# Seven block products for queries, keys and values, in a planned two-layer graph kernel

## The chip, the cores and the metric

The kernel runs on one core of a Trainium2 chip. The metric is device time in microseconds. The engines are named as in the profile: PE is TensorE (matmuls, with PEld for its weight loads), DVE is VectorE, ACT is ScalarE, POOL is GpSimd, and SP is SyncE, which here issues all DMAs.

## The reference

There are 64 graphs of 256 nodes with 256 features, all in float32, and an adjacency matrix for each. Two layers follow each other.

```
layer 0:  two graph attentions (softmax over axis 1 of masked pairwise scores, times h @ W),
          residual, layer norm, feed-forward 256 -> 1024 -> 256 with ReLU, residual, layer norm
layer 1:  q, k = x @ Wq + bq, x @ Wk + bk             (8 heads of 32)
          out = sum over r of (softmax(q k^T / sqrt(32)) * (adj == r)) @ (x @ Wv[r] + bv[r])
          x = LN(x + out @ Wo + bo);  x = LN(x + gelu(x @ W1 + b1) @ W2 + b2)
```

The adjacency holds only 0 and 1, so only two of the four value matrices matter.

## The kernel before

The graphs are taken in 32 pairs. `whole_way(pair)` is a Python generator that emits the instructions of one pair: `gat_layers` (both graph attentions), `feed_forward` stage 0, `attention`, `feed_forward` stage 2, and the store. What reaches PE is cut into steps: each `yield` names the events that the next step needs, what it must hold alone ("gat", "ff", "attention"), and how many PSUM banks and other buffers it takes. Work for the other engines is given to `put(engine, us, emit, *events, rank=..., needs=..., frees=...)`.

`run(reliefs(), ways, 3)` is a planner. It keeps a clock for each engine, costs that are written beside each piece, and lists of when buffers come free (`free`). With three pairs in flight it always emits the piece that can start first; on PE it prefers a step that has been ready for 0.5 us, oldest pair first. `keep_order` then pins each engine to the emitted order. So the order is fixed when the program is built, and each engine is an in-order queue: an instruction that waits holds up all behind it on its engine. The true waits are semaphores.

The lines that matter below, by the work they do:

- L409, L425, L438: matmuls of the graph attentions; L400 and L380 evacuate and scale on ACT.
- L589: first half of the feed-forward network. `Slabs` computes a product of 2 x 2 blocks with seven block products (the Winograd form of Strassen's scheme) in place of eight. For two slabs of 128 rows it uses three banks: `x` collects products 1, 6, 7 and 4, and is copied out by ACT (L595) after 1, 6 and 7; `w` holds product 2, `z` products 5 and 3. DVE adds at L601, and makes the sums of input blocks at L560. L576 is the activation.
- L674: second half of the feed-forward network; L451, L463 to L479: residual and layer norm, with the root on POOL (L469, L470) and the normalisation on ACT (L474).
- L499, L504, L510: the rows are turned into columns by a DVE transpose into `yb`, a store and four gathers. In the first and last pairs ("hurried") PE does it (L530, L534).
- L695: queries and keys, two matmuls of 512 columns each for two halves of the features. L687: values, in the same way for each half of a graph. L696 and L689 evacuate with the bias.
- L728: scores by head; L735 exp on ACT; L739 and L743 mask and add halves on DVE; L757 and L760 products with the values and the sums of the softmax; L769 and L770 divide; L766 adds the divisor and its reciprocal up into `reach`, a check of the range that is read at the end.
- `load(pair)` starts DMAs for xT, the adjacency and x of the next pair. The adjacency becomes bytes on ACT (L393) and gives a maximum on DVE (L396).
- `relieve`, `relieve_values` and `block_sums` prepare biases and block sums of weights once, at the start.

If the check of ranges failed, `any_inputs` would do everything anew by another way; with these inputs it doesn't run.

Of the kernel before, what the change touches and what calls it, by code (L numbers as in the profile page):

```python
# [10 lines left out]
F32 = mybir.dt.float32  # L11
# [7 lines left out]
P = 128  # L19
# [9 lines left out]
BY_BLOCKS = (0, 2)  # L29
# [4 lines left out]
def two_layers(ctx: ExitStack, tc: tile.TileContext, t: dict, out: bass.AP, flag: bass.AP):  # L34
# [37 lines left out]
    reach = const.tile([P, NPAIR, 2 * KC], F32, name="reach")  # L72
# [49 lines left out]
    small = ctx.enter_context(tc.tile_pool(name="small", bufs=4))  # L122
# [3 lines left out]
    def bank():  # L126
# [12 lines left out]
    free = {name: [0.0] * n for name, n in (("bank", 8), ("a", 2 * HQ), ("m", 2 * HQ), ("h", 2 * HQ), ("yb", 2), ("yT", 2), ("yTa", 1),  # L139
                                             ("xT", 1), ("rows", 1), ("e", 2), ("adjT", 1), ("adj", 3), ("sums", 1), ("x", 4))}  # L140
# [69 lines left out]
    def run(besides, ways, together):  # L210
# [5 lines left out]
        while True:  # L216
# [8 lines left out]
            for n, (way, events, name, banks, *more) in enumerate(going):  # L225
                if alone.get(name) in (None, way) and all(e.time is not None for e in events):
                    at = begins(max([e.time for e in events], default=0.0), "bank" if banks else None, banks)
                    for needs in more:
                        at = None if at is None else begins(at, needs)
                    if at is not None:  # L230
                        times.append((at, n))
# [8 lines left out]
            if engine == "tensor":  # L240
                sure = [n for at, n in times if at <= now - SLACK]
                g = going[min(sure, key=lambda n: (going[n][2] == "ff" or alone.get("ff") is going[n][0], n))
                          if sure else min(times)[1]]
                if g[2]:
                    alone[g[2]] = g[0]
# [32 lines left out]
    def load(pair, at=None):  # L278

        to, rows = {}, slice(2 * pair, 2 * pair + 2)  # L280

        def xT():
            to["xT"] = io.tile([P, KC, 512], F32, name="xT")
            nc.sync.dma_start(to["xT"], t["xT"][pair].rearrange("(c p) b n -> p c (b n)", p=P))

        def adjT():
            if pair == 1:
                to["adjT"] = work.tile([P, 2, 2 * D], F32, name="v", bufs=2).bitcast(I32).rearrange(
                    "p b (c n) -> p (b c) n", c=2)
            else:  # L290
                to["adjT"] = io.tile([P, 4, N], I32, name="adjT")
            nc.sync.dma_start(to["adjT"], t["adjT"][rows].rearrange("b (c p) n -> p (b c) n", p=P))

# [3 lines left out]

        if at is None:
            return to, [put("sync", 0.45, emit, rank=3, lag=2.3, kb=512, needs=emit.__name__) for emit in (xT, adjT, x)]
        for emit in (xT, adjT, x):  # L300
            takes(emit.__name__, pair == 0 or emit is x)
            emit()
        return to, [at_time(at)] * 3
# [56 lines left out]
    def gat_weights(y, at, at_home, ratio, there, to, empty, b):  # L360
# [3 lines left out]
        def weigh(j):  # L364
# [7 lines left out]
            nc.vector.scalar_tensor_tensor(e[:, j], to["adj"][:, k], empty[:, k:k + 1], e[:, j],  # L372
# [13 lines left out]
    def gat_layers(pair, to, loads):  # L386
        yield loads[:1], "gat", 2
        empty = small.tile([P, 4], F32, name="empty")
        y = work.tile([P, 4, D + 4], F32, name="xw", bufs=2)

        def small_adj():
            to["adj"] = io.tile([P, 4, N], U8, name="adj", bufs=3)
            nc.scalar.activation(to["adj"], to["adjT"], AF.Copy)  # L393

        def largest():
            nc.vector.tensor_reduce(most[:, pair], to["adjT"].bitcast(U32), axis=AX.X, op=ALU.max)  # L396
            nc.vector.tensor_scalar(empty, most[:, pair], 0.0, EVEN, ALU.is_le, ALU.mult)
# [5 lines left out]
        emptied = put("vector", 1.35, largest, put("scalar", 1.2, small_adj, loads[1], needs="adj"), rank=2, frees=["adjT"] * (pair != 1))  # L403
# [10 lines left out]
        frees_at(clock["tensor"], ["xT"] * (pair > 0))  # L414
        at_home, ratio, there = yield from addends(y, there, D + 2, 0, pair)
        e = [gat_weights(y, D + 2, at_home, ratio, [emptied, *there], to, empty, b) for b in range(2)]
# [14 lines left out]
        e = [gat_weights(z, D, at_home, ratio, there, to, empty, b) for b in range(2)]  # L431
        normal = {}
        for b in range(2):
            yield [e[b][1]], None, 1
# [54 lines left out]
    def transposed(y, ready, to, b, pair, stage):  # L489
# [6 lines left out]
        def turn():  # L496
            nonlocal blocks
            blocks = work.tile([P, 8, 2, 32], F32, name="yb", bufs=2)
# [40 lines left out]
    def feed_forward(y, normal, w, func, relieved, gb, pair, stage):  # L539

# [3 lines left out]
        half, by_blocks = NF // 2, stage in BY_BLOCKS  # L546
        sums = p2 = None
        f, evacuated = [], [[None] * NF for _ in range(2)]

        def block(c, k):  # L550
            return normal["yT"].rearrange("p b a (c k i) -> p c k (b a) i", c=KC, k=2)[:, c, k]

        def sum_of_blocks(n):
            nonlocal sums
            if n == 0:
                sums = work.tile([P, 3, N], F32, name="sums_yT")
            t1, t2, t4 = (sums[:, n].rearrange("p (a i) -> p a i", i=32) for n in range(3))
            to, of, less = ((t1, block(0, 1), block(0, 0)), (t2, block(1, 1), t1),
                            (block(0, 1), block(1, 1), block(0, 1)), (t4, block(1, 0), t2))[n]
            nc.vector.tensor_tensor(to, of, less, ALU.subtract)  # L560

        if hurried(pair, stage):
            yield from transposed_on_tensor(y, normal)
        if by_blocks:
            summed = [put("vector", 0.34, lambda: sum_of_blocks(0), normal[0], normal[1], rank=0, needs="sums")]
            for n in range(1, 4):
                summed.append(put("vector", 0.34, lambda n=n: sum_of_blocks(n), summed[-1], rank=0))

        def slabs():

            tile = work.tile([P, 2, 512], F32, name="ff", bufs=NF // 2)
            f.extend(tile[:, n] for n in range(2))
            return tile

        def activate(to, p, m, us, *events, rank=0, frees=()):
            return put("scalar", us, lambda: nc.scalar.activation(to, p, func, bias=b1[:, m:m + 1]), *events, relieved,  # L576
                       rank=rank, function=kind, frees=frees)

        class Slabs:

            def __init__(self, t):
                self.t, self.bank, self.there = t, {}, {}

            def product(self, n, to, of, rhs, first=False):

                if first:
                    self.bank[to] = bank().rearrange("p (n c) -> p n c", n=2)
                for n in range(2):
                    nc.tensor.matmul(self.bank[to][:, n], lhsT=w1[:, of, (self.t + n) * P:(self.t + n + 1) * P], rhs=rhs(),  # L589
                                     start=first and n == 0, stop=True, skip_group_check=True)  # L590
                return took(0.86)

            def evacuate(self, name, rows, at, event):
                def copy():
                    nc.scalar.activation(self.rows[rows][:, :, at], self.bank["x"], AF.Copy)  # L595
                self.there[name] = put("scalar", 0.5, copy, event, rank=-1)

            def add(self, name, rows, at, bank, *events, frees=()):
                def add():
                    to = self.rows[rows][:, :, at]  # L600
# [756 lines left out]
```

## Time and profile before

| | |
|---|---|
| median of 3 runs | 3093.85 us (3093.08 to 3093.98) |
| profiled execution | 3093.45 us, span 3091.7 us |
| granted clock of PE | 0.995 |
| DMA | 205.6 MB, mean 67 GB/s |

A row of the page's groups reads: line, engine, operation, written tile <- read tiles, shape and count, then busy time, the mean of one in ns, and the idle time just before them with what ended it. A matmul of float32 data appears as two records. "Busy" counts a moment once if any instruction of the engine runs.

### The profile page before, as it was taken

What the parts mean: (1) busy time and instruction counts of PE and PEld (TensorE: products, weight loads), DVE (VectorE), ACT (ScalarE), POOL (GpSimd) and SP (SyncE); (2) the same over time, 40 slices, a digit from 0 to 9 for tenths busy, and PEclk for the clock granted to TensorE, in tenths of its full rate; (3) what the DMA queues carried; (4) which work ended last, traced back from release to release, by engine and by line L of the source; (5) the groups of instructions that cost most, each with busy time, mean ns of one, the idle gap of its engine ahead of it and who ended that gap; (6) DMA issues with size and microseconds to landing.
All of it is one profiled execution on the core that took longest, in us unless ns stands there. A gap on an engine that the chain in (4) does not pass through costs nothing. (4 is left out here: it accounts for less than half of the span.)

```text
span 3091.7 us, 50645 instructions
## 1 busy us (share of the span) xinstructions
PE 3052.6 (99%) x18366; PEld 2309.3 (75%) x18366; DVE 2465.3 (80%) x5917; ACT 1622.4 (52%) x3452; POOL 265.9 (9%) x518
## 2 busy tenths in 40 slices
PE   7999999999999999999999999999999999999997
PEld 6777876886687778668867876786688678767856
DVE  5788888878887878888788878888887888788775
ACT  4455654653565456546545654564465456545534
POOL 0001100000010001001000100010010001000100
PEclk8999999999999999999999999999999999999999
DMA  6112311230132123113201311231132113112200
GB/s 193 38 37 65 123 35 42 90 103 29 62 101 64 35 69 117 38 39 97 95 33 58 104 61 35 76 110 44 33 102 90 35 56 110 55 40 64 69 1 15
DMA packets 210496, 205.63 MB, mean 67 GB/s; under 512 B 22208, under 2 KB 169792, under 8 KB 210240
## 3 DMA queue, kind: packets, MB, share of 16 engines
q1 hardware_dynamic: 210240, 202.32, 20.3%
q8 instruction: 148, 2.42, 0.3%
q14 instruction: 108, 0.88, 0.1%
HBM read 137.51 MB, written 64.73 MB: 65 GB/s over the span
## 5 line engine op out<-in xcount | busy, mean ns | idle before, releaser
L474 ACT ACTIVATE x<-x,less,rstd 128x256 f32<-128x256 f32 x512 | 279.1, 593 | 416.0 <-POOL less L470 414.6
L735 ACT ACTIVATE a<-ps 128x512 f32<-128x512 f32 x512 | 272.3, 603 | 395.2 <-PE ps L728 395.1
L674 PE MATMUL ps<-w_L_gnn_w_ff,ff 128*128 128x256 f32 x2048 | 462.6, 381 | 0.0
L674 PE MATMUL ps<-w_L_gnn_W,ff 128*128 128x256 f32 x2048 | 458.7, 380 | 1.7 <-ACT ff L576 1.7
L469 POOL TENSOR_TENSOR rstd<-rstd,mhalf 128x2 f32<-128x2 f32 x256 | 206.2, 806 | 2797.2 <-DVE less L466 2598.4
L674 PEld LDWEIGHTS ps<-w_L_gnn_w_ff,ff 128*128 128x128 f32 x2048 | 386.5, 190 | 70.8 <-issue 20.7
L674 PEld LDWEIGHTS ps<-w_L_gnn_W,ff 128*128 128x128 f32 x2048 | 388.2, 190 | 66.4 <-issue 12.9
L739 DVE TENSOR_TENSOR m<-a,adj 128x512 f32<-128x512 f32 x512 | 349.9, 683 | 81.8 <-ACT a L735 80.5
L595 ACT ACTIVATE ff<-ps 128x512 f32<-128x512 f32 x384 | 223.4, 590 | 220.9 <-PE ps L589 220.2
L769 DVE RECIPROCAL s<-ps 128x256 f32<-128x256 f32 x128 | 224.4, 1753 | 139.2 <-PE ps L760 139.1
L601 DVE TENSOR_TENSOR ff<-ps,ff 128x512 f32<-128x512 f32 x384 | 249.0, 681 | 26.4 <-PE ps L589 19.7
L589 PE MATMUL ps<-yT,w_L_gnn_W1p 128*128 128x256 f32 x1024 | 248.3, 386 | 4.5 <-ACT a L735 2.0
L687 PE MATMUL ps<-wv,yTa 128*128 128x512 f32 x512 | 238.7, 599 | 0.0
L589 PE MATMUL ps<-yT,w_L_gnn_w_ff1p 128*128 128x256 f32 x1024 | 238.3, 381 | 0.3 <-ACT ff L595 0.2
L451 DVE TENSOR_TENSOR x<-ps,x 128x512 f32<-128x512 f32 x256 | 174.7, 683 | 71.8 <-PE ps L674 42.6
L589 PEld LDWEIGHTS ps<-yT,w_L_gnn_W1p 128*128 128x128 f32 x1024 | 192.2, 191 | 46.1 <-ACT ff L595 5.7
L589 PEld LDWEIGHTS ps<-yT,w_L_gnn_w_ff1p 128*128 128x128 f32 x1024 | 193.3, 190 | 30.9 <-DVE x L451 3.3
L463 DVE BATCH_NORM_STATS2 st<-x 128x6 f32<-128x256 f32 x512 | 209.3, 409 | 5.5
L743 DVE TENSOR_TENSOR h<-a 128x256 f32<-128x256 f32 x512 | 213.5, 417 | 0.0
L400 ACT ACTIVATE xw<-ps 128x260 f32<-128x260 f32 (+1 forms) x256 | 96.7, 388 | 171.6 <-PE ps L425 91.4
L687 PEld LDWEIGHTS ps<-wv,yTa 128*128 128x128 f32 x512 | 94.7, 190 | 120.3 <-issue 120.1
L589 PE MATMUL ps<-sums_yT,w_L_gnn_w_ff1p 128*128 128x256 f32 x768 | 180.6, 381 | 0.4 <-DVE sums_yT L560 0.4
(118 smaller groups left out, 4743.6 us busy)
## 6 DMA issues: line engine op xcount, KB each, us to landing
home<-yb SPq DMA_DIRECT2D x182, 256.0 KB, 2.0
yT<-home SPq DMA_DIRECT2D x728, 64.0 KB, 2.0
rows<-row SPq DMA_DIRECT2D x60, 512.0 KB, 3.9
xT<-in_xT SPq DMA_DIRECT2D x32, 512.0 KB, 3.7
x<-in_x SPq DMA_DIRECT2D x32, 512.0 KB, 4.1
out<-x SPq DMA_DIRECT2D x32, 512.0 KB, 2.9
adjT<-in_adjT SPq DMA_DIRECT2D x31, 512.0 KB, 4.1
w_L_gnn_w_ff1p<-in_L_gnn_w_ff1p SPq DMA_DIRECT2D x4, 256.0 KB, 5.6
```

What stands on the lines that cost most here:

```text
L463: nc.vector.bn_stats(st[:, j, :], rows[j])
L469: nc.gpsimd.tensor_tensor(rstd, rstd, mhalf[:, :2], ALU.pow)
L474: nc.scalar.activation(rows[j], rows[j], AF.Identity, bias=less[:, j:j + 1], scale=rstd[:, j:j + 1])
L589: nc.tensor.matmul(self.bank[to][:, n], lhsT=w1[:, of, (self.t + n) * P:(self.t + n + 1) * P], rhs=rhs(), start=first and n == 0, stop=Tru ...
L595: nc.scalar.activation(self.rows[rows][:, :, at], self.bank["x"], AF.Copy)
L601: nc.vector.tensor_tensor(to, self.bank[bank], to, ALU.add)
L674: nc.tensor.matmul(p2[:, j * D:(j + 1) * D], lhsT=f[m][:, (2 * j + b) * P:(2 * j + b + 1) * P], rhs=w2[:, m, :], start=m == 0, stop=m == N ...
L687: nc.tensor.matmul(ps, lhsT=yT[:, b, c, jc * P:(jc + 1) * P], rhs=wv[:, c].rearrange("p r m -> p (r m)"), start=c == 0, stop=c == KC - 1)
L735: nc.scalar.activation(a[n][o], ps[o], AF.Exp)
L739: nc.vector.tensor_tensor(m[n][o], a[n][o], adj, ALU.mult)
L743: nc.vector.tensor_tensor(h[n][o], a[n][o][:, :N], a[n][o][:, N:], ALU.add)
L769: there = put("vector", 1.68, lambda: nc.vector.reciprocal(s, po[:, N:]), there, rank=0)
```

## The change

Queries and keys are now one 2 x 2 block product, values another, both by the seven-product scheme that the feed-forward network uses. The scheme moves into two classes: `Second` makes the sums of the input's blocks (the fourth one in place, once both readers of the block have run), `Blocks` holds the seven steps. Its fifth product goes into the bank of the second one after C11 has been read out, so two slabs need four banks and not six. Four pairs are in flight in place of three. xT and the adjacency share one input buffer, adjacency first. `yb` has one buffer in place of two, the small tiles three in place of four. The check of ranges moves from DVE to ACT, and the divisor takes the place of a tile `h`.

```diff
-    small = ctx.enter_context(tc.tile_pool(name="small", bufs=4))
+    small = ctx.enter_context(tc.tile_pool(name="small", bufs=3))
...
-    free = {name: [0.0] * n for name, n in (("bank", 8), ("a", 2 * HQ), ("m", 2 * HQ), ("h", 2 * HQ), ("yb", 2), ("yT", 2), ("yTa", 1),
-                                             ("xT", 1), ("rows", 1), ("e", 2), ("adjT", 1), ("adj", 3), ("sums", 1), ("x", 4))}
+    free = {name: [0.0] * n for name, n in (("bank", 8), ("a", 2 * HQ), ("m", 2 * HQ), ("h", 2 * HQ), ("yb", 1), ("yT", 2), ("yTa", 1),
+                                             ("input", 1), ("rows", 1), ("e", 2), ("adj", 4), ("sums_yT", 1), ("sums_yTa", 1), ("x", 4))}
...
+        def in_bytes(there):
+            return put("vector", 1.35, largest, put("scalar", 1.2, small_adj, there, needs="adj", rank=2), rank=2)
...
         if at is None:
-            return to, [put("sync", 0.45, emit, rank=3, lag=2.3, kb=512, needs=emit.__name__) for emit in (xT, adjT, x)]
+            adj = in_bytes(there(adjT, needs="input"))
+            return to, [there(xT, adj), adj, there(x, needs="x")]
...
+    class Second:
...
+        def add(self, n):
+            if n == 0:
+                self.sums = work.tile([P, 2, N], F32, name=self.name)
+            b, (t1, t2) = self.b, (self.sums[:, n].rearrange("p (a i) -> p a i", i=32) for n in range(2))
+            to, of, less = ((t1, b(0, 1), b(0, 0)), (t2, b(1, 1), t1), (b(0, 1), b(1, 1), b(0, 1)), (b(1, 0), b(1, 0), t2))[n]
+            nc.vector.tensor_tensor(to, of, less, ALU.subtract)
...
+    class Blocks:
...
+        def product(self, n, to, a, first=False):
+            if first:
+                self.bank[to] = self.bank[to] if n == 5 else bank().rearrange("p (n c) -> p n c", n=2)
+            for slab in range(2):
+                self.multiply(self.bank[to][:, slab], slab, a, self.second.of(n),
+                              start=first and slab == 0, stop=True, skip_group_check=True)
+            return took(0.86)
...
+        def p1(self):
+            yield *self.first, 1
+            self.begin()
+            self.u1 = self.copy(0, 0, self.product(1, "x", 0, True))
+        def p2(self):
+            yield [], None, 1
+            there = self.product(2, "z", 1, True)
+            self.c11 = self.add(0, 0, "z", self.u1, there)
+            self.second.read_by_second(there)
+        def p5(self):
+            yield [self.c11, self.second.there[0]], None, 0
+            self.fifth = self.product(5, "z", 2, True)
+            self.add_fifth()
+        def p6(self):
+            yield [self.u1, self.second.there[1]], None, 0
+            self.u2 = self.copy(0, 1, self.product(6, "x", 3))
+        def p7(self):
+            yield [self.u2, self.second.there[2]], None, 0
+            self.u3 = self.copy(1, 1, self.product(7, "x", 4))
+            self.add_fifth()
...
+        def p4(self):
+            yield [self.u3, self.second.there[3]], None, 0
+            self.corner(self.bank["x"], self.product(4, "x", 6))
+        def p3(self):
+            yield [self.c22], None, 0
+            self.add(0, 1, "z", self.u2, self.product(3, "z", 5), frees=["bank"])
...
-            blocks = work.tile([P, 8, 2, 32], F32, name="yb", bufs=2)
+            blocks = work.tile([P, 8, 2, 32], F32, name="yb")
...
-            for step in (a.p1, b.p1, a.p2, a.p6, b.p6, a.p5, b.p5, a.p7, b.p7, b.p2, a.p4, b.p4, a.p3, b.p3):
+        for step in (a.p1, b.p1, a.p2, a.p6, b.p2, b.p6, a.p5, a.p7, b.p7, b.p5, a.p4, b.p4, a.p3):
...
+        def multiply_qk(to, n, a, b, **flags):
+            nc.tensor.matmul(to, lhsT=wqk[:, a, n * P:(n + 1) * P], rhs=b, **flags)
+        def multiply_v(to, jc, a, b, **flags):
...
+            nc.tensor.matmul(to, lhsT=b[:, jc * P:(jc + 1) * P], rhs=wv[:, a], **flags)
...
             def check():
-                nc.vector.scalar_tensor_tensor(s, po[:, N:], 1.0, s, op0=ALU.mult, op1=ALU.add,
-                                               accum_out=reach[:, pair, n:n + 1])
+                for of, c in ((s, 0), (po[:, N:], 1)):
+                    nc.scalar.activation(of, of, AF.Copy, accum_out=reach[:, pair, c, n:n + 1])
...
-        ready = [[projected(qT, 0, yT, wq, bqs, SCALE)], []]
...
+        for step in (a_.p1, b_.p1, a_.p2, a_.p6, b_.p2, a_.p5, b_.p6, a_.p7, b_.p5, a_.p4, b_.p7, lambda: scores(0), a_.p3, b_.p4,  b_.p3, lambda: scores(1)):
+            yield from step()
...
-    run(reliefs(), (whole_way(pair) for pair in range(NPAIR)), 3)
+    run(reliefs(), (whole_way(pair) for pair in range(NPAIR)), 4)
```

In the last list `a_` is the product for queries and keys, and `b_` the one for values. Their weights come by twelve DMAs in place of four, and at the start DVE also scales the query weights and makes the sums of their blocks. In `feed_forward` the last step, `b.p3`, is put behind the first matmuls of the second half.

## The prediction

> **What bounds the kernel now.** I read the page first: busy time of the engines, then the slices.
>
> ```profile
> span 3091.7 us, 50645 instructions
> PE 3052.6 (99%) x18366; PEld 2309.3 (75%) x18366; DVE 2465.3 (80%) x5917; ACT 1622.4 (52%) x3452; POOL 265.9 (9%) x518
> ```
>
> TensorE looks full, but busy matmul records overlap, so I asked for busy time by stretches (columns: length, then busy us of PE, PEld, DVE, ACT, POOL, clock, DMA share, GB/s).
>
> ```profile
> 0.00:77.00 77.00, 60.79 (x335) 51.00 (x336) 41.90 (x128) 32.89 (x85) 2.49 (x10) 0.89 0.63 193
> 77.00:2950.00 2873.00, 2870.49 (x17079) 2172.22 (x17078) 2330.70 (x5581) 1532.83 (x3262) 253.03 (x488) 1.00 0.20 66
> 2950.00:3092.00 142.00, 121.36 (x956) 86.04 (x954) 92.69 (x210) 56.66 (x106) 10.41 (x20) 0.95 0.03 9
> ```
>
> Of 39 us without a matmul, 16 lie in the first 77 us and 21 in the last 142. In the 2873 us between them 2.5 us are missing: there every us of TensorE work taken away is a us of time, unless a wait takes its place. So I need true prices of matmuls, from start to start in the timeline of PE (start, length, line, tiles, records; one float32 matmul leaves two records).
>
> ```profile
> 1024.82 1.88 PE L695 MATMUL ps<-yTa,w_L_gnn_Wqp 128*128 128x512 f32 x4
> 1026.53 1.88 PE L695 MATMUL ps<-yTa,w_L_gnn_Wkp 128*128 128x512 f32 x4
> 1028.25 1.88 PE L687 MATMUL ps<-wv,yTa 128*128 128x512 f32 x4
> 1030.06 1.15 PE L728 MATMUL ps<-qT,kT 32*128 32x256 f32 x16
> ...
> 1058.55 2.86 PE L589 MATMUL ps<-yT,w_L_gnn_W1p 128*128 128x256 f32 x12
> 1061.24 3.62 PE L589 MATMUL ps<-sums_yT,w_L_gnn_W1p 128*128 128x256 f32 x16
> 1065.03 1.13 PE L589 MATMUL ps<-yT,w_L_gnn_W1p 128*128 128x256 f32 x4 [0.17 <-ACT ff L595]
> ```
>
> Two 512-column matmuls take 1.71 to 1.81 us, 0.43 to 0.45 a record. The 256-column ones of the feed-forward network, which run the same seven-product scheme already, take 2.69/12 = 0.224 and, without the 0.17 wait, 3.62/16 = 0.226; over three windows of 100 us I get 0.440 and 0.2205. The price goes by columns. The last row also shows what a late evacuation costs under this scheme: 0.17 us. The waits of PE confirm it: on the evacuation at L595, 1.9 us in 11 times over the whole run.
>
> [...] the costliest PE group has records of 381 ns in 463 us for 2048, 226 each. Hence the start-to-start prices.
> [...]
>
> **The change, part by part.**
>
> *TensorE.* Removed per pair: 8 matmuls at L695 and 8 at L687, all of 512 columns: 1024 records x 0.440 = 451 us. Added: 7 products x 2 halves x 2 kinds = 28 of 256 columns per pair: 1792 records x 0.2205 = 395 us. **Minus 56 us**; 49 to 65 with 0.2245 and 0.2155 for the new ones. The feed-forward product count stays. Nothing hides this: it is on the path for 2873 us.
>
> *VectorE.* Added per pair: four sums of blocks (256 columns, 418 ns) and six additions (three for queries and keys, three for values; 512 columns, 681 ns): 5.8 us. Removed: the check at L766, 405 + 82 ns, four times: 1.95 us. The four value evacuations stay. Net 3.8 us, 122 us in all; DVE goes to 2590 us, 85% of the new span, 87% in the steady stretch. It still fits behind TensorE on average. Cost on the path: nothing where other pairs' products cover; without that cover see the third case.
>
> *ScalarE.* Queries and keys: 8 evacuations of 256 columns instead of 4 of 512: 8 x 0.47 (L576 from PSUM) - 4 x 0.69 = +1.0 us a pair. The check: 8 copies of 256 columns with an accumulator; no row shows ACT reading one. [...]I take 0.5 with the read (0.4 to 0.7): +4 us a pair. In the planned order of ACT's instructions the changes between exp and gelu number 66 before (the groups by line show 33 + 20 + 12 + 1 table loads) and 98 after, each 1.28: +41 us. Together some 200 us: 60% busy. Behind TensorE; but a table load now stands more often ahead of an evacuation.
>
> *Waits inside the new block.* From the planned order of matmuls I worked out what lies between a product and the one that needs its evacuation: at least 1.76 us (two products) everywhere. Two ACT evacuations take 0.94, a DVE addition 0.68[...]: 0.4 to 0.7 to spare, less than one 1.75 us reciprocal (L769) or one table load in front. I charge 0.2 us a pair, as L595 shows, +6; bounds 0 and 30.
>
> *Four pairs, four banks.* A fourth pair gives more matmuls to fill with; in steady state only 2.5 us can be won. The slabs hold four banks instead of six. Both reach the ends only: bounds -6 and +6, taken as 0.
>
> *Smaller buffers.* yb 2 to 1: a transpose waits for the store of the one before, 2.0 us to landing; behind it on DVE stand masks and layer norms. 182 transposes of 0.7 us stand some 16 us apart, but two of a pair come within 3.5 us. Small tiles 4 to 3: a layer norm is open for some 3.6 us (L463 at 43.35 to the end of L474 at 46.9). 0 taken, up to +15.
>
> *Start.* SP issues 15 weight DMAs for attention instead of 7, at least 0.43 us each, with the queue full anyway: +1 to +4 us on everything behind them. For the third pair the adjacency now comes before its xT, in one buffer: DMA, ACT conversion 1.05, DVE maximum 1.21, then xT. xT was issued at 40.5 and first used at 61.7, so its detour (4 + 2.3 + 4 us) is covered. But in ACT's new order the conversion stands ahead of the first layer norm (it ran at 45.8), and the adjacency, issued at 41 to 45 with 5.9 us to landing, is there at 47 to 51: 2 to 5 us lost on the first pair's chain, when nothing else is ready. VectorE also gets 12 small sums (4 us) by 60 us. **+4**, 0 to 10.
>
> *End.* The last pair runs alone as now, with one more dependence (the fifth product after C11, five products later): 0, -4 to +6. The chain of what ended last is two DVE additions at L479, unchanged.
>
> Sum: -56 + 6 + 4 = -46 on the profiled execution's 3093.45 (span 3091.7): 3047. The median of the runs shown is 0.4 higher, so I take 3047 for the median too.
>
> **The rivals.** What no measurement here would tell from no change is 0.2%, 6 us.
> 1. *TensorE stays the bound* (0.74): 3047, with its own bounds 3030 to 3066. For it: 2.5 us of waits now, under the same scheme.
> 2. *Half is given back* (0.17): products wait 0.2 us at each of four or five evacuations of the block, because ACT at 60% and DVE at 87% have something in front: some 0.9 us a pair, 28 us more: 3075. For it: slack of 0.4 us. Against: some sixteen dependences of this kind per pair cost 1.9 us over the whole run today.
> 3. *VectorE sets the pace in the attention block, and it gets slower* (0.07). Between the first new product and the first L757 products, TensorE has 12.3 us of projections and 2.2 of scores. VectorE has four sums, six additions, four evacuations and eight masks and halves, at 0.35 and 0.62 us back to back: 1.4 + 3.7 + 2.5 + 7.7 = 15.3 us, where now 9.0 lie (two evacuations, the same masks). Other pairs' VectorE work adds to that. If those products come late and the pairs at hand run out of covered matmuls, each pair loses the excess. From 1.75 us a pair (56/32) the gain is gone; at 3 us the time is 3093 - 56 + 96 = 3133. Against: 28 us of L674 matmuls per feed-forward pass need little of VectorE and can stand there.
> 4. *No difference* (0.02): the same with 1.6 to 1.9 us a pair.
>
> **How the numbers follow.** Case 1 gives the time, 3047. The range takes case 1's lower bound, 3030, and nearly all of case 2: 3080; left out are case 3 and the tails. Faster 0.91, same 0.02, slower 0.07.
>
> **What would show it.** Right: PE without a matmul under 15 us between 77 us and the last 150; the new 256-column rows at 0.215 to 0.225 a record; DVE near 2590 us, ACT near 1820, 98 table loads; in the first 80 us some 20 us without PE. Wrong: waits of PE on the new additions or evacuations over 30 us in sum, a DVE above 92% in steady state, waits of DVE on the store of yb, or 256-column products above 0.23 a record.

## The result, and the profile after

| | median | range | ratio to before |
|---|---|---|---|
| before | 3093.47 us | 3091.9 to 3093.98 (4 runs) | |
| after | 3070.78 us | 3069.0 to 3072.0 (4 runs) | 0.9927, 95% interval 0.991 to 0.9944 |

The change saves 22.7 us, a little under half of the forecast 46. The first lines of the page after:

```profile
span 3067.2 us, 52833 instructions
PE 3008.9 (98%) x19138; PEld 2461.4 (80%) x19138; DVE 2565.5 (84%) x5993; ACT 1805.6 (59%) x4124; POOL 251.5 (8%) x518
```

The spans differ by 24.5 us. TensorE is busy for 43.7 us less than before (3052.6 to 3008.9), and without a matmul for 19.2 us more (39.1 to 58.3). The busy time by stretches (length, then PE, PEld, DVE, ACT, POOL, clock, DMA share, GB/s) shows where those are:

```profile
0.00:77.00 77.00, 57.42 (x297) 49.00 (x298) 42.04 (x131) 28.83 (x74) 2.49 (x10) 0.78 0.57 174
77.00:2925.00 2848.00, 2828.15 (x17929) 2314.07 (x17929) 2433.66 (x5664) 1698.67 (x3894) 237.42 (x486) 1.00 0.21 67
2925.00:3068.00 143.00, 123.30 (x915) 98.32 (x913) 89.83 (x201) 78.13 (x156) 11.54 (x22) 0.93 0.04 12
```

In the middle, 19.9 us are now missing, where 2.5 were before; the forecast had given under 15. The start misses 19.6 (16.2 before), the end 19.7 (20.6). The middle's loss is early. Between 300 and 500 us, the windows of the kernel before and then of the changed one read:

```profile
300.00:500.00 200.00, 200.00 (x1119) 154.52 (x1117) 161.97 (x397) 108.25 (x233) 18.02 (x36) 1.00 0.23 75
```

```profile
300.00:500.00 200.00, 192.28 (x1180) 156.47 (x1180) 172.63 (x422) 127.30 (x284) 18.17 (x36) 0.99 0.25 80
```

That is 7.7 us in 200, and the next 500 us miss 5.8 more (0.5 before). The waits of PE over the whole run (line <- what ended the wait: us in total, times, longest) are:

```profile
PE ps L677 <- ACT ff L683: 9.5, 11, 2.2
PE pw L117 <- DVE junk L111: 7.6, 1, 7.6
PE ps L645 <- DVE x L594: 7.1, 2, 5.8
PE ps L460 <- ACT rise L447: 4.1, 1, 4.1
PE ps L553 <- ACT xw L505: 3.9, 1, 3.9
PE ps L540 <- ACT xw L505: 3.9, 2, 2.9
PE ps L677 <- DMA yT<-home: 3.6, 1, 3.6
PE ps L708 <- ACT ff L689: 2.5, 2, 1.6
```

The long ones at L117, L460, L553, L540 and L645 lie mostly in the first 77 us or in the last 60. Between 300 and 1000 us 13.5 us are missing (0.5 before), and the longest entries are these, first after, then the only one before:

```profile
PE ps L677 <- ACT ff L683: 4.6, 6, 2.2
PE ps L677 <- DMA yT<-home: 3.6, 1, 3.6
PE ps L708 <- ACT ff L689: 1.6, 1, 1.6
```

```profile
PE ps L589 <- ACT ff L595: 0.3, 2, 0.2
```

All entries at L677 together are 10.1 of the 13.5 us. The new products, L750 and L755, do not appear. One of the waits at L677, on ACT's timeline and then on PE's:

```profile
435.38 1.28 ACT L447 ACT_TABLE_LOAD   x1
436.67 0.30 ACT L447 ACTIVATE rise<-xw,shift 128x4 f32<-128x4 f32 x1
436.88 0.29 ACT L448 ACTIVATE rise<-xw,shift 128x4 f32<-128x4 f32 x1
437.07 0.19 ACT L449 ACTIVATE ratio<-xw 128x4 f32<-128x4 f32 x1
437.17 1.06 ACT L683 ACTIVATE ff<-ps 128x512 f32<-128x512 f32 x2
```

```profile
437.80 1.13 PE L677 MATMUL ps<-sums_yT,w_L_gnn_w_ff1p 128*128 128x256 f32 x4 [2.19 <-ACT ff L683]
```

ACT runs another pair's table load and three small operations first, 1.8 us, and the copy for which PE waits 2.19 us stands behind them. L677 is the first half of the feed-forward network (L589 before, which waited 1.9 us on the same evacuation over the whole run). The forecast price of its products and of the new ones was nearly right, as PE's timeline from 1024 us shows, with products of three kinds taking turns:

```profile
1024.39 1.03 PE L750 MATMUL ps<-yTa,wqk 128*128 128x256 f32 x4
1025.25 1.03 PE L755 MATMUL ps<-wv,yTa 128*128 128x256 f32 x4
1026.11 1.03 PE L750 MATMUL ps<-yTa,wqk 128*128 128x256 f32 x4
1026.98 1.03 PE L677 MATMUL ps<-yT,w_L_gnn_w_ff1p 128*128 128x256 f32 x4
1027.84 1.03 PE L750 MATMUL ps<-sums_yTa,wqk 128*128 128x256 f32 x4
```

From 1024.39 to 1027.84 are 16 records in 3.45 us: 0.216 a record. The record itself lasts 0.38, so a matmul that is late by less than 0.16 leaves no gap; busy time hides such waits. To count them too I subtracted from the time the matmuls' own price, every record at its start-to-start price where nothing waits (0.216 for 256 columns, 0.429 for 512, some 0.054 for the records of attention that use 32 rows or columns). What remains, in us, is a count of this kind over all records of five traces ("order", with SLACK at 0.46, and "light", without the gain and with ReLU, are experiments below):

| stretch, us | before | after | eight products | after, other order | after, light |
|---|---|---|---|---|---|
| price of all matmuls | 2955.3 | 2903.0 | 2958.3 | 2903.0 | 2903.0 |
| above it, 0 to 77 | 38.4 | 46.1 | 44.0 | 46.0 | 45.6 |
| 77 to 300 | 8.0 | 8.0 | 6.4 | 8.2 | 6.2 |
| 300 to 1000 | 16.4 | 37.0 | 19.5 | 28.1 | 25.3 |
| 1000 to 2900 | 52.6 | 55.9 | 51.2 | 56.7 | 49.2 |
| 2900 to the end | 20.8 | 17.4 | 6.4 | 18.3 | 13.2 |

So the matmuls got 52.3 us cheaper, and 28.2 came back: 7.7 at the start, 20.6 between 300 and 1000 us, 3.3 later, less 3.4 at the end. Counted by line between 300 and 1000 us, the time above the price just before products of L677 is 18.3 us (5.0 before, at L589), and before those of L750 and L755 together 2.6 (5.0 before, at L695 and L687). So the new block has no waits hidden in busy time either. After that middle stretch the order repeats itself every five pairs, 463.1 us (the same wait of 1.17 us on L683 stands at 1187.49 and at 1650.60): 92.6 us a pair, against 282.3 for three pairs, 94.1, before. That part gives 1.5 us a pair, as a saving of 48 us in all would.

### The profile page after: what moved, and what is told of

Its sections match the earlier page's. It is cut to its first block, busy times and chain, and to the rows that moved or that the text cites. A ratio compares the mean times of both kernels' runs of the same rounds, so it can differ in the third digit from the quotient of the medians.

```text
span 3067.2 us, 52833 instructions
## 1 busy us (share of the span) xinstructions
PE 3008.9 (98%) x19138; PEld 2461.4 (80%) x19138; DVE 2565.5 (84%) x5993; ACT 1805.6 (59%) x4124; POOL 251.5 (8%) x518
## 5 line engine op out<-in xcount | busy, mean ns | idle before, releaser
L589 ACT ACTIVATE x<-x,less,rstd 128x256 f32<-128x256 f32 x512 | 278.1, 593 | 317.4 <-POOL less L585 316.8
L584 POOL TENSOR_TENSOR rstd<-rstd,mhalf 128x2 f32<-128x2 f32 x256 | 192.1, 750 | 2787.3 <-DVE less L581 2604.1
L677 PE MATMUL ps<-yT,w_L_gnn_W1p 128*128 128x256 f32 x1280 | 314.3, 385 | 12.8 <-ACT ff L683 6.6
L677 PE MATMUL ps<-yT,w_L_gnn_w_ff1p 128*128 128x256 f32 x1280 | 307.9, 381 | 1.4 <-ACT ff L683 0.7
L683 ACT ACTIVATE ff<-ps 128x512 f32<-128x512 f32 x384 | 223.0, 590 | 123.6 <-PE ps L677 121.8
L677 PEld LDWEIGHTS ps<-yT,w_L_gnn_W1p 128*128 128x128 f32 x1280 | 240.1, 191 | 61.3 <-ACT ff L683 13.1
L677 PEld LDWEIGHTS ps<-yT,w_L_gnn_w_ff1p 128*128 128x128 f32 x1280 | 241.2, 190 | 42.2 <-ACT ff L683 6.2
L833 DVE RECIPROCAL h<-ps 128x256 f32<-128x256 f32 x128 | 222.6, 1746 | 44.7 <-PE ps L824 44.2
L765 ACT ACTIVATE qk<-ps,bqk 128x256 f32<-128x256 f32 x256 | 107.0, 469 | 189.5 <-PE ps L750 189.5
L689 ACT ACTIVATE ff<-ff,c_L_gnn_b_ff 128x256 f32<-128x256 f32 x384 | 173.8, 504 | 45.1 <-DVE ff L388 44.5
L689 ACT ACTIVATE ff<-ff,c_L_gnn_b 128x256 f32<-128x256 f32 x384 | 170.4, 502 | 40.9 <-DVE ff L388 39.6
L750 PE MATMUL ps<-yTa,wqk 128*128 128x256 f32 x640 | 167.7, 384 | 0.0
```

Source lines behind the costliest of these rows:

```text
L584: nc.gpsimd.tensor_tensor(rstd, rstd, mhalf[:, :2], ALU.pow)
L589: nc.scalar.activation(rows[j], rows[j], AF.Identity, bias=less[:, j:j + 1], scale=rstd[:, j:j + 1])
L677: nc.tensor.matmul(to, lhsT=w1[:, a, (t + slab) * P:(t + slab + 1) * P], rhs=b, **flags)
L683: return put("scalar", 0.5, lambda: nc.scalar.activation(target(c, h), blocks.bank["x"], AF.Copy), event, rank=-1)
L689: evacuated[h][m] = put("scalar", 0.4, lambda m=m, to=to, source=source: nc.scalar.activation(to, source, func, bias=b1[:, m:m + 1]), even ...
L833: there = put("vector", 1.68, lambda: nc.vector.reciprocal(s, po[:, N:]), there, rank=0)
```

## Experiments

All ratios are to the kernel before, run on the same chip, whose medians were 3092.2 to 3092.9 us. Single runs of one kernel lie 2 to 7 us apart (10 with three pairs in flight), and differences to "after" compare medians from different chips. So a difference of 2 or 3 us says nothing, and sums of two or three differences are good to a few us. Where the number of pairs, the products or the banks change, the planner also writes another order of turns.

### Which part of the change does what

**Eight products.** The product is made by eight 256-column products; sums and six additions fall away. Everything else of the change stays. Of the edit, the order of the steps:

```diff
-        for step in (a_.p1, b_.p1, a_.p2, a_.p6, b_.p2, a_.p5, b_.p6, a_.p7, b_.p5, a_.p4, b_.p7, lambda: scores(0), a_.p3, b_.p4,  b_.p3, lambda: scores(1)):
+        for step in (eight("qk", 0, 0), eight("qk", 1, 0), eight("v", 0, 0), lambda: scores(0), eight("v", 1, 0), eight("qk", 0, 1),
+                     lambda: scores(1), eight("qk", 1, 1), eight("v", 0, 1), eight("v", 1, 1)):
```

> The changed kernel with queries, keys and values by eight block products of 256 columns again, without sums of blocks and additions; four pairs, four banks for the feed-forward slabs, one input buffer and the small buffers stay. By the price of matmuls this costs 55 us. If the new block's load on ACT and DVE causes the 17 us of new waits, these go and the time is about 3109 (38 us slower than the changed kernel). Rival (the waits come from the feed-forward order, the fourth pair or the buffers): they stay, 3124 or slower.

Measured: 3089.24 us, ratio 0.999 (0.9983 to 0.9996). Its steady waits nearly go:

```profile
300.00:500.00 200.00, 198.47 (x1071) 167.65 (x1070) 156.65 (x411) 125.15 (x287) 18.86 (x38) 1.00 0.29 92
```

All the rest of the change together is worth 3 us, in which the start costs 5.6 and the end gives 14.4 (the table above). Both numeric expectations missed: the time was expected 20 us or more above this. The seven products alone give 18.5 us of the 55.3 that their matmuls cost less (2958.3 to 2903.0), so 37 us of loss come with them, or with the order that the planner writes for them: 17.5 between 300 and 1000 us, and 11.0 at the end (17.4 against 6.4), where the wait at L645 of 7.1 us for the last layer norm, in the list above, is missing with eight products. Most of the loss at the start (5.6 of 7.7 us) is there with eight products too.

**Three pairs in flight.**

```diff
-    run(reliefs(), (whole_way(pair) for pair in range(NPAIR)), 4)
+    run(reliefs(), (whole_way(pair) for pair in range(NPAIR)), 3)
```

> The changed kernel with three pairs in flight in place of four; nothing else. If the fourth pair is what brings the late evacuations (98 table loads; here the order has 72), the waits of PE between 77 us and the last 150 fall from 19 us to some 5 and the time to about 3058. Rival (the fourth pair is cover that the seven-product block needs): waits grow to 40 us or more, 3090 or slower.

Measured: 3224.32 us, ratio 1.0423 (1.0409 to 1.0437). Its waits of PE:

```profile
PE ps L553 <- ACT xw L505: 54.8, 22, 4.2
PE ps L677 <- DMA yT<-home: 27.2, 13, 4.5
PE ps L677 <- ACT ff L683: 20.7, 19, 3.0
```

With three pairs the changed kernel takes 154 us more than with four. Without the fourth pair the change would have cost time. That it is the seven products which need the cover is likely but not shown: no run has eight products with three pairs, and the second entry, the transposed tile, may come from the single buffer `yb`.

**Six banks for two slabs.** The second product gets a bank of its own, so that the fifth needn't wait for C11, in both places where the scheme is used.

```diff
-            self.c11 = self.add(0, 0, "z", self.u1, there)
+            self.c11 = self.add(0, 0, "w", self.u1, there, frees=["bank"])
...
-                self.bank[to] = self.bank[to] if n == 5 else bank().rearrange("p (n c) -> p n c", n=2)
+                self.bank[to] = bank().rearrange("p (n c) -> p n c", n=2)
...
-            yield [self.c11, self.second.there[0]], None, 0
+            yield [self.second.there[0]], None, 1
```

> The changed kernel with a bank of its own for the second product again, so six banks for two slabs, in the feed-forward network and for queries, keys and values; the fifth product then needn't wait for C11. If the four banks make the waits on ACT's evacuations at the feed-forward products, they fall by half and the time to about 3062. Rival (banks are scarce with four pairs): steps wait for banks and the time is 3080 or slower.

Measured: 3095.07 us, ratio 1.0007 (0.9999 to 1.0015): 24 us more than with four. The loss is not in the early stretch: between 1000 and 2900 us 29.1 us are missing, where 5.5 were with four. In these orders, the banks saved are worth more than the dependence on C11 costs.

### The start

The first feed-forward product starts at 66.18 us before and at 75.10 after, with the same matmuls done ahead of it. Two things are late. First, SP issues the first pair's adjacency only at 11.13 us in place of 3.57, since the tile `v` it goes into shares its memory with the setup's tiles. Second, ACT in its order after:

```profile
53.57 1.06 ACT L299 ACTIVATE adj<-input 128x1024 uint8<-128x1024 int32 x1 [8.54 <-DMA input<-in_adjT]
54.53 1.57 ACT L589 ACTIVATE x<-x,less,rstd 128x256 f32<-128x256 f32 x3
```

ACT waits 8.54 us for the third pair's adjacency, and the first layer norm stands behind it: it runs at 54.53, and ran at 45.82 before.

**First cause alone**: the first pair's adjacency goes into a buffer for x.

```diff
-                to["adjT"] = work.tile([P, 2, 2, 2 * D], F32, name="v")[:, pair].bitcast(I32).rearrange(
-                    "p b (c n) -> p (b c) n", c=2)
+                to["adjT"] = (io.tile([P, 4, D], F32, name="x", bufs=4).bitcast(I32) if pair == 0 else work.tile(
+                    [P, 2, 2, 2 * D], F32, name="v")[:, pair].bitcast(I32).rearrange("p b (c n) -> p (b c) n", c=2))
```

> The changed kernel, but the first pair's adjacency is loaded into one of the four x buffers, which is free from the start, and no longer into the value tile v. Theory: v shares its memory with the tiles of the setup, so SP holds the load back until the setup's matmuls have read them (11.1 us in place of 3.6), and all of ACT's first work waits behind it; then the first feed-forward product moves from 75 us to about 67 and the time falls by 8 us, to 3063. Rival (the start is late because of eight more weight DMAs and the conversion ahead of the layer norm): under 3 us, 3068 to 3071.

Measured: 3068.78 us, 0.9924 (0.991 to 0.9937). The first product starts at 72.07, 3.0 us earlier; the 2.0 us in the time are within the spread of the runs. The earlier wait went, but the wait of ACT for the third adjacency grew to 11.13 us: the second cause took over, and the expected 8 us did not come.

**Both causes**: also tell the planner that SP is busy until 48 us, which puts the normalisation ahead of that conversion.

```diff
-START = {"tensor": 12.0, "vector": 11.0, "scalar": 12.0, "gpsimd": 0.0, "sync": 40.0}
+START = {"tensor": 12.0, "vector": 11.0, "scalar": 12.0, "gpsimd": 0.0, "sync": 48.0}
```

> The start alone: the first pair's adjacency goes into a buffer for x, and the planner takes SP as busy until 48 us in place of 40, so that ScalarE's conversion of the third pair's adjacency is put behind the first layer norm's normalisation and not ahead of it. The first experiment removed the first cause alone and gained 2 us. If the two causes at the start are the whole of it: the first feed-forward product at 66 to 68 us as in the kernel before (75 in the changed one), the time 3062 to 3064. Rival, something third is late at the start (the sums of blocks of the weights on VectorE, or the weights' own DMAs): first product at 70 or later, 3067 to 3071.

Measured: 3066.27 us, 0.9915 (0.9902 to 0.9929). ACT's order is turned round, and the first layer norm runs at 47.58:

```profile
47.58 1.09 ACT L589 ACTIVATE x<-x,less,rstd 128x256 f32<-128x256 f32 x2 [6.37 <-POOL less L585]
```

The first product starts at 66.41, as before the change. The time falls by 4.5 us (the five runs lie between 3062.85 and 3069.23, so its size is rough), less than the 7 to 9 expected: this first product is now followed by others' matmuls, and the next of its kind comes at 71.64. The start's loss has these two causes, and some 4 us of it (42.5 above the price at 77 us, against 38.4) remain with a cause not shown.

### Load on VectorE and ScalarE

Here the changed kernel keeps its order, and work is taken away or replaced. Without the gain or with ReLU it no longer computes the whole reference.

```diff
-            for v, op in ((g, ALU.mult), (beta, ALU.add)):
+            for v, op in ((beta, ALU.add),):
...
-                for of, c in ((s, 0), (po[:, N:], 1)):
-                    nc.scalar.activation(of, of, AF.Copy, accum_out=reach[:, pair, c, n:n + 1])
+                pass
...
-    small = ctx.enter_context(tc.tile_pool(name="small", bufs=3))
+    small = ctx.enter_context(tc.tile_pool(name="small", bufs=4))
...
-                        to, source, func, bias=b1[:, m:m + 1]), event, rank=h - 1, function=kind,
+                        to, source, AF.Relu, bias=b1[:, m:m + 1]), event, rank=h - 1, function=kind,
```

The expectations are those of the first, second, third and fourth edit alone, and of the first and fourth together:

> The changed kernel in exactly its order, but the layer norms leave out the multiplication by the gain: 256 DVE instructions of 512 columns less, some 160 us of DVE (2565 to about 2410), more than the change added. If DVE, busy for 87% of the steady stretch, is what makes the evacuations late, most of the 28 us of added slack on PE goes: 3050 or faster. Rival (ACT or the DMAs are late): 3066 to 3070.

> The changed kernel in exactly its order, but the check of ranges is left out: 256 ACT copies with their accumulator reads less, some 150 us of ACT in pieces of 1.1 us. If the check on ACT stands in front of evacuations that PE waits for, 6 to 15 us go: 3055 to 3064. Rival (it stands in gaps): 3068 to 3071.

> The changed kernel in exactly its order with four buffers for the small tiles in place of three. If layer norms hold each other up by their small tiles, 3 to 10 us go. Rival, which I hold likelier: no difference, 3068 to 3072.

> The changed kernel in exactly its order, but the second layer's activation is ReLU in place of GELU, so that ACT never changes its table: 97 loads of 1.28 us less, 124 us of ACT. Three of the five longest waits of PE on ACT that I looked at had a table load in front. If the loads make the evacuations late, 10 us or more go: 3060 or faster. Rival: the next thing in the queue is late instead, 3066 to 3070.

> The changed kernel's own order, with the multiplication by the layer norm's gain left out and GELU replaced by ReLU, so with no change of tables and 155 us less on VectorE and some 125 us less on ScalarE; output accordingly. Each alone gave 14.6 and 6.8 us. If the two loads delay TensorE at different moments: the sum, 21 us, 3049. If both relieve the same waits: 15 to 16 us, 3055. What then still lies above the predicted 3047 can't be load on these engines and is in the order or the start.

| run | us | ratio (interval) | against after |
|---|---|---|---|
| without the gain (DVE 2411 us) | 3056.15 | 0.9881 (0.9866 to 0.9896) | -14.6 |
| without the check | 3070.87 | 0.993 (0.9917 to 0.9944) | +0.1 |
| four small tiles | 3070.18 | 0.9929 (0.9915 to 0.9942) | -0.6 |
| ReLU for GELU (ACT 1682 us) | 3064.02 | 0.9908 (0.9893 to 0.9923) | -6.8 |
| without the gain, and ReLU | 3044.93 | 0.9847 (0.9833 to 0.986) | -25.9 |

The check on ACT and the smaller pool cost nothing that these runs can tell. The gain alone and ReLU alone each fell between their two forecasts. The two loads together give 25.9 us, more than their sum of 21.4. In this last trace the waits of PE on L683 fall from 9.5 us to 1.0:

```profile
PE ps L677 <- ACT ff L683: 1.0, 4, 0.3
```

But that doesn't show that the change *brought* 26 us of loss, since a lighter VectorE could help any kernel of this kind. Two controls take the same loads away elsewhere.

> The kernel before, in its own order, with the two loads taken away: no multiplication by the layer norm's gain, ReLU in place of GELU; output accordingly. The same edit gave the changed kernel 26 us. If that relieves what the change brought (its products wait for evacuations, additions and sums that stand behind other work), the kernel before, with 2.5 us of waits in its steady part, gains only at its start and end: 3085 to 3091. If a lighter VectorE and ScalarE help any kernel of this kind alike: 3067 to 3073, and the 26 us say nothing of the change.

> The kernel with eight products and the rest of the change, with the same two loads taken away; output accordingly. Against the changed kernel without them (3045) it gives what seven products for eight are worth when VectorE and ScalarE have room; with the loads it was 18 us of the 55 that the matmuls take. If the loss is the load standing before the new evacuations and additions: 3080 to 3088 here, so 35 to 43 us. If it is the loads in general: 3063, so 18 us again.

| | with the loads | without | difference |
|---|---|---|---|
| before | 3092.9 | 3078.77 (0.9962, 0.9948 to 0.9975) | -14.1 |
| eight products | 3089.24 | 3073.43 (0.9938, 0.9924 to 0.9951) | -15.8 |
| after | 3070.78 | 3044.93 (0.9847, 0.9833 to 0.986) | -25.9 |

Both expectations missed: the truth is between. Some 15 us are what each of these three kernels gains; about 10 to 12, good to some 3 us, belong to the seven products. With light engines those are worth 28.5 us (3073.43 to 3044.93), with the loads 18.5. So load explains some 10 of the 37 us lost, not all of it.

**Load without dependence.** The eight-product kernel gets two operations on VectorE, whose result nobody reads, behind each value evacuation (edit against the eight-product kernel).

```diff
                 nc.vector.tensor_tensor(target_v(r, b), of_v.bank["x"] if ps is None else ps, bias, ALU.add)
+                nc.vector.tensor_tensor(dummy, dummy, dummy, ALU.mult)
+                nc.vector.tensor_tensor(dummy[:, :N], dummy[:, :N], dummy[:, :N], ALU.mult)
```

> The kernel with eight products in place of seven and the rest of the change (3089 us), in its own order, with two more operations on VectorE behind each of the four value evacuations of a pair, 512 and 256 columns on a tile that nothing else reads: 1.1 us each, 141 us in all, as much as the sums and additions of the seven-product scheme cost there. No product waits for them. Theory load (VectorE's fullness alone delays the evacuations for which TensorE waits): 3103 to 3110. Theory dependence (the scheme loses because its own products must wait for additions and sums, and turns between the pairs with them): 3089 to 3093.

Measured: 3094.53 us, 1.0007 (0.9998 to 1.0015), with DVE busy for 2433.9 of the first 2925 us (2325.7 without them): 5.3 us more, between the two theories and nearer to the second. The operations came to 108.1 us there; 141 were expected over the whole run. A busier VectorE that nothing new waits for costs little at this place. That fits a loss from the load together with products that wait for it, but one place for the load is not a proof.

### The order of the turns

The planner fixes the order by its own clock, and by that clock it already foresees moments in which none of the four pairs has a matmul ready. Near 361 us one waits for its transposed tile, one for masks, the others for their turn in the feed-forward network or in attention. Read while the kernels are built, this clock has the matmuls wait 16.2 us between 300 and 1000 us in the changed kernel, 1.8 in the kernel before and 4.3 with eight products. So 14.4 us of the middle's loss of 20.6 already stand in the plan, which knows the other engines only by the costs written in the kernel. **Another order**: one number of the planner, which sets from when the oldest pair's step is preferred.

```diff
-SLACK = 0.5
+SLACK = 0.46
```

> One number of the planner is changed, SLACK from 0.5 to 0.46 us (how long a step must have been ready before the oldest pair's step is preferred). Instructions, operands and buffers stay the same; from about 300 us on the order in which the four pairs take their turns differs. By the planner's own clock the matmuls wait 2.6 us in place of 10.6 between 300 and 500 us, and as long as before elsewhere. Theory A, the 20 us that the changed kernel loses between 300 and 1000 us lie in this written order: 3062, some 8 us under the changed kernel's 3070. Theory B, they come from VectorE and ScalarE being fuller: no difference, 3068 to 3072. Rival: the 0.04 us only move the wait to a place the planner doesn't see: 3070 or more.

Measured: 3064.0 us, 0.991 (0.9895 to 0.9925): 6.8 less than after, with the same instructions. The stretch that had missed 7.7 us:

```profile
300.00:500.00 200.00, 196.98 (x1212) 161.63 (x1212) 172.77 (x425) 124.15 (x281) 20.88 (x40) 1.00 0.25 80
```

Now 3.0 us are missing. Between 300 and 1000 us the time above the price falls by 8.9 us (37.0 to 28.1), and by the planner's clock 8.0 were to go. A part of the middle loss is an accident of the written order.

**Truer costs for the planner**, with the start as above.

```diff
-            put("scalar", 1.0, check, there, frees=["bank", "h"])
+            put("scalar", 1.2, check, there, frees=["bank", "h"])
...
-        there = put("vector", 1.22, statistics, *events)
+        there = put("vector", 1.3, statistics, *events)
...
-        return put("vector", 1.2, scale, put("scalar", 0.8, normalise, there))
+        return put("vector", 1.2, scale, put("scalar", 0.9, normalise, there))
```

> The start of the run before this one, and a planner that takes three steps at nearer to what the trace shows: the check 1.2 us in place of 1.0, the statistics of a layer norm 1.3 in place of 1.22, its normalisation 0.9 in place of 0.8. Same instructions, another order from about 200 us on. By the planner's own clock the matmuls wait 3.3 us between 300 and 500 us in place of 10.6, and 52 in all in place of 56. If the loss lies in an order planned with too low costs: 3050 to 3058. If a plan with true costs gives no better order: the time of the run with the start alone, within 4 us.

Measured: 3068.79 us, 0.9929 (0.9916 to 0.9943), no better than the start alone (3066.27). The stretch from 300 to 500 us is better there too (196.1 busy), and other stretches give it back: from 1000 to 2900 us 13.7 us are missing, where 5.5 were after. Costs that are nearer to the trace did not make a better order here.

**Start and order together.**

> The two edits that each helped, together: the first pair's adjacency in a buffer for x and SP taken as busy until 48 us (4.5 us alone), and SLACK 0.46 (6.8 us alone). By the planner's own clock 2.6 us of waits between 300 and 500 us again in place of 10.6. If the start and the order are two separate losses: 3059.5, within 3 us. If the time won at the start is lost again in the order (the pairs then only meet earlier): 3064 or more.

Measured: 3059.49 us, 0.9894 (0.9879 to 0.9909). Within the spread of the runs the two add up (4.5 + 6.8), and this is the fastest kernel here that computes the whole reference: 11 us under the changed one, 33 under the one before.

**And without the two loads.**

> The same, with the gain's multiplication left out and ReLU in place of GELU, as in the run with both loads taken away; output accordingly. If start, order and load are three separate losses: 3045 less 11, so 3034. If the order's loss was a wait for the same late evacuations: 3040 or more. By the matmuls alone, with the kernel before's own waits, it would be 3093 less 56 and less what the lighter load would have given there.

Measured: 3041.35 us, 0.9832 (0.9818 to 0.9845): 3.6 us under the same without the fixes, where 11 were to be won. Between 300 and 1000 us the time above the matmuls' price is 25.6 us, as with the loads gone alone (25.3). So the gain of the other order is gone when the engines are light: the two look like mostly the same loss seen twice. The likely reading, not shown by itself, is that a tight place in the order hurts when the evacuation is late.

## Why the prediction was wrong, and where it was right

- **TensorE, -56: nearly right.** By the matmuls' own prices it is -52.3. The prices 0.440 and 0.2205 were averages over 100 us with other waits in them; rows where nothing waits give 0.429 and 0.216, a ratio of 1.99.
- **VectorE, ScalarE: sizes right.** DVE 2565.5 us (2590 forecast), ACT 1805.6 (1820), 98 table loads (98), 1.28 us each. The 418 and 681 ns taken for VectorE's operations are those of L560 and L601 in the trace before. The 0.5 us for a copy of the check with its read was my estimate; the two kinds took 0.61 and 0.56 (last section). For VectorE, "Cost on the path: nothing where other pairs' products cover" did not hold throughout: of the loss against eight products, some 10 us go when the two engines are lighter.
- **Waits inside the new block, +6: the step that failed.** The block itself has no wait on its evacuations: L750 and L755 are not among the waits. The cover that I counted there held. Some 0.4 us of it I had given to the ways between the engines, an estimate that the trace doesn't show: in the kernel before, an ACT that waits for a matmul starts 0.04 us after the matmul's modelled end (median of 515 waits), and a matmul that waits for ACT 0.05 us after ACT's end (17 waits). With these, "0.4 to 0.7 to spare" is 0.7 to 1.0, and the "slack of 0.4 us" that spoke for the second case is not measured. I didn't ask what the seven products do to the products of *other* pairs. With the change the feed-forward products at L677 wait, behind a table load as at 435.38, or for a late transposed tile (3.59 us at 378.06). The term for waits should have been some 24 us (20.6 between 300 and 1000, 3.3 after), where 6 stood. Its evidence was also read too low: the gap of 0.17 us at L595 is only the visible part. From 1061.24 to 1065.03 are 3.79 us, and the 16 records between cost 3.46 at 0.216, so that product was late by 0.33. The 1.9 us of waits at L595, and the 2.5 us in all, leave out what busy time hides.
- **Four pairs, 0: wrong reason.** That "only 2.5 us can be won" was read off the kernel before. The changed kernel needs the fourth pair (154 us), and the four banks (24 us). A wait list of the old kernel doesn't tell what the new one needs. That the whole rest of the change with eight products gives only 3 us makes the 0 look right, by luck.
- **Smaller buffers, 0: right for the small tiles** (0.6 us, no difference). VectorE now waits 20.2 us in 18 times for the store of `yb`, one of the prediction's signs of being wrong. The eight-product kernel has the single `yb` too, without the middle's loss (19.5 us above the price between 300 and 1000 us, 37.0 after), so the single buffer alone doesn't make that loss; no run gives the second one back.
- **Start, +4: mechanism right, size too small.** The conversion did stand ahead of the first layer norm. The second cause, a tile whose memory comes free late, was missed. The "at least 0.43 us" for an issue is too high: in the trace before, those of attention's weights and biases take 0.37 (`wv`) to 1.25 us (`b_L_gnn_bv`). And SP issues for 23.1 of the 32.3 us from 11.78 to 44.08, so "the queue full anyway" is not shown. Measured +7.7, of which the low clock is a part (granted 0.78 in the first 77 us, 0.89 before). Between 57 and 68 us, for example, the granted clock is 0.5, and most of the 16 records of 258 columns from 63.25 to 69.60 us, 0.40 each on average, fall in there; later such records take 0.218. The matmuls that ran at half the clock in the first 80 us are worth 11.4 us at full price, 6.6 before. If each took double, the clock is some 5 of the 7.7 us, by this estimate. No run separates it from the waits.
- **End, 0:** -3.4, within its bounds; with eight products it is -14.4.

The measured steps give -52.3 + 23.9 + 7.7 - 3.4 = -24.1, the spans -24.5. In size this is the second case, "half is given back" (3075), but not by its mechanism: it put the waits at the new evacuations. The third case did not come: no wait at L821 is in the list. What is shown is that the loss comes with the seven products and their order, that most of its middle part stands at L677, and that another order or lighter engines take part of it away. What stays open: in 300 to 1000 us the light kernel with either order still loses some 9 us against the light eight-product one (25.3 or 25.6 to 16). It goes with the products' dependences and turns, and no run shows by which.

## What to carry to other kernels

Here the matmuls saved paid less than half, because products that the change doesn't touch came to wait. So after costing the new block, ask of *every* old product what it waits for in the new order. In a kernel with a written order, treat the order as part of the change: a small number in the planner was worth 6.8 us here, beside 22.7 for the whole change. Ask the planner's own clock for its waits in the old and the new order first: 1.8 and 16.2 us between 300 and 1000 us could be read before the kernel ran. And run a control on the kernel before for every load that is taken away; without it 26 us would have been put down to the change, where 10 to 12 belong to it.

## What the runs showed of the hardware

Reading ACT's accumulator is an instruction of its own, here half as long as the copy that fills it. In the groups of ACT after:

```profile
L831 ACT ACTIVATE h<-h 128x256 f32<-128x256 f32 x128 | 53.5, 418 | 150.2 <-DVE qk L834 150.2
L831 ACT ACTIVATE ps<-ps 128x256 f32<-128x256 f32 x128 | 47.9, 374 | 0.0
L831 ACT ACTIVATION_READ_ACCUMULATOR h<-h 128x1 f32 x128 | 25.0, 195 | 0.0
L831 ACT ACTIVATION_READ_ACCUMULATOR ps<-ps 128x1 f32 x128 | 24.2, 189 | 0.0
```

One check is 418 + 195 + 374 + 189 = 1176 ns, where the planner's cost was 1.0 us; without it the time was the same within the spread of the runs, so no cost of it on the path can be seen.
